# Four edits to a two-layer metaformer kernel: the last image in two halves, additions in place of reductions, a residual by load, and first loads in another order

## The chip, the cores and the metric

The kernel runs on one core of a Trainium2 chip. The metric is the device time of one execution in microseconds, lower is better. A core has five engines with a queue of instructions each: PE (TensorE, matrix products into PSUM), DVE (VectorE), ACT (ScalarE), POOL (GpSimd) and SP (SyncE, which only issues transfers here). Each works through its own queue in order and waits on semaphores of the others. Transfers (DMA) are issued from SP, ACT or POOL.

## What is computed

x is 8 x 128 x 32 x 32 in fp32: 8 images, 128 channels, 1024 positions ("tokens"). Two layers, each with a mixer and a feed-forward part, both with a residual:

```python
# layer 0
x = x + attention(_ln_c(x))                  # 8 heads, softmax over 1024 tokens
t = _to_tokens(x)
t = t + stu(_ln_t(t))                        # causal convolution with 16 spectral filters, then
x = _from_tokens(t, x)                       # einsum('btkd,k,kde->bte'), plus 3 lags; 4 resolutions
# layer 1
x = x + deformable_conv(_ln_c(x))            # per token 3 taps, each 4 corners, bilinear weights and a mask
t = _to_tokens(x)
t = t + experts(_ln_t(t))                    # softmax router over 8 experts, the best 2, normalised
x = _from_tokens(t, x)
```

In the deformable convolution a tap reads four table rows at computed places and adds them with weights:

```python
samp = gather(iy0, ix0) * (1 - wy) * (1 - wx) + gather(iy0, ix0 + 1) * (1 - wy) * wx + ...
samp = samp * mask[:, j][..., None]
out = out + jnp.einsum('bhwc,oc->bohw', samp, conv_w[:, :, 0, j])
```

## The kernel before

**Stages.** Attention for all 8 images comes first. Then `spectral_and_second_layer` runs the STU of layer 0 and, interleaved with it by hand, layer 1. The order of instructions on each engine is the order in which this Python code emits them.

**The STU.** The work is a list of 128 units (8 images x 16 filters). For each unit `filter_image` makes the convolution (products `p_x`, `p_y`, `p_z` on PE, put together by ACT, POOL and DVE into `us`), and two units later `mix` multiplies `us` by the filter's matrix `mf` and adds the product into `po`, an accumulator in PSUM that holds one image. `start_sums` opens `po` at the first filter of an image: 8 products with `flip`, a reversed identity, put the residual x1 into it (L1437, with the matmul in `add`, L1453). `x1` holds the image's tokens in reversed order; a gather brings it in `prepare` (L1391), and two buffers alternate. At an image's end `finish` copies `po` into `x2`, one half on ACT (L1529), one on DVE (L1530).

Before the first unit SP issues, in this order, the filters of units 1 and 2 (`teto`, L1257 and L1258), the matrices of the lags (`mu`, L1322) and the parts of the first mixing matrix (`m_room`, L1366). From `m_room` POOL forms `both` (L1371, L1372), and from it DVE the matrix `mf` (L1379, L1381). `setup` of layer 1 then loads small weights, the last step of which adds a bias to the table of base positions (L906).

**Layer 1.** The class `DeformAndExperts` has two generators. Each `yield` hands back an amount of time, and after each half of a unit `advance(RATE)` lets the generators go on by 3.2 such units (`LAST_RATE`, 3.6, during the last image). `points` turns the image back to tokens (`turn_back`: 4 transposes into a PSUM bank, a copy by ACT to `tok`, L1168 and L1169; twice), normalises it (`norm_steps`, with `inverse_std`: three Newton steps in small instructions), turns it again (L919), multiplies by the taps' weights (`p_g`, L1025), copies to `gs` on ACT (L1028) and writes `gs` to a table in DRAM, 24 writes of 256 KB (L1018): 3 taps x 4 corners x 2 halves of the image. Offsets and masks (`p_om`, `corners`) give the row numbers and the weights `w`. `sampled` then works on tiles of 128 tokens, 8 for an image. For a tile 3 gathers (L1077, by POOL) bring 12 x 128 values into `g`; taps 0 and 1 are weighted on ACT (L1095, 8 instructions), tap 2 on DVE (L1099); then DVE adds up the 12 parts and `tok`:

```python
nc.vector.tensor_reduce(x3[:, i, :], g.rearrange("p t k c -> p c (t k)"), AX.X, ALU.add)   # L1103
nc.vector.tensor_add(x3[:, i, :], x3[:, i, :], tok[:, i, :])                               # L1106
```

After the 8 tiles come a normalisation, a turn (L919), the router (`gates`: logits `p_l` L1180 on PE, about 20 small instructions on DVE, L1186 to L1209) and, tile by tile, the experts: two products `p_e` (L1123), gates on four experts by ACT (L1130) and four by DVE (L1135), the sum of 8 parts by a reduction (L1140) and an addition (L1143). After four tiles a bank `p_out` (L1152, L1155) is copied to `ot`, and at the end one transfer writes the image (L1160). Tiles `g` of both steps share three buffers.

The layer-1 work of an image runs behind its STU, inside the STU of the next one. For the last image there is no next one: after the last unit a loop lets `layer.image(B - 1, ...)` run alternately with what is left of the rows. There `alone` is true: the Newton steps are on DVE instead of POOL, and every second table write is issued by ACT (L1017).

Of the kernel before, what the change touches and what calls it, by code (L numbers as in the profile page):

```python
# [11 lines left out]
F32 = mybir.dt.float32  # L12
I32 = mybir.dt.int32
# [5 lines left out]
P = 128  # L19
# [16 lines left out]
LAST_RATE = 3.6  # L36
# [726 lines left out]
def inverse_std(nc, pool, var, eps, newton):  # L763


    v = pool.tile([P, NT], F32, tag="rs_v", name="rs_v", bufs=2)
    y = pool.tile([P, NT], F32, tag="rs_y", name="rs_y", bufs=2)
    t = pool.tile([P, NT], F32, tag="rs_t", name="rs_t", bufs=2)
    bits = pool.tile([P, NT], I32, tag="rs_b", name="rs_b", bufs=2)
# [33 lines left out]
class DeformAndExperts:  # L803
# [4 lines left out]
    def __init__(  # L808
        self, ctx, tc, ident, dram, conv_w, conv_b, off_w, off_b, mask_w, mask_b,
# [6 lines left out]
        self.ident, self.dram, self.out = ident, dram, out  # L816
# [4 lines left out]
    def setup(self):  # L821
# [13 lines left out]
        bias = cp.tile([P, 9], F32, name="bias")  # L835
# [64 lines left out]
        for i in range(NT):  # L900
# [5 lines left out]
        nc.vector.tensor_tensor(  # L906
            self.base, self.base, bias.unsqueeze(1).to_broadcast([P, NT, 9]), ALU.add
# [17 lines left out]
    def first_max(self, e, name):  # L925

        nc = self.nc
        top = self.sb.tile([P, NT], F32, tag="top", name=f"top_{name}")
        oh = self.sb.tile([P, NT, NE], F32, tag=f"oh_{name}", name=f"oh_{name}")
        nc.vector.tensor_reduce(top, e, AX.X, ALU.max)  # L930
        nc.vector.tensor_tensor(oh, e, top.unsqueeze(2).to_broadcast([P, NT, NE]), ALU.is_equal)
        nc.vector.scalar_tensor_tensor(oh, oh, -64.0, self.eidx, ALU.mult, ALU.add)
        nc.vector.tensor_reduce(top, oh, AX.X, ALU.min)
        nc.vector.tensor_tensor(oh, oh, top.unsqueeze(2).to_broadcast([P, NT, NE]), ALU.is_equal)
        return oh
# [49 lines left out]
    def image(self, b, x2):  # L985

        got = []
        yield from self.points(b, x2, got, True)
        yield from self.sampled(b, got, True)

    def points(self, b, x2, got, alone):
# [5 lines left out]
        yield from self.turn_back(x2, tok)  # L997
# [15 lines left out]
        def write():  # L1013
            if writes:
                i0, tap, slot, back = writes.pop(0)
                r0 = 33 - back + i0 * P
                queue = nc.scalar if alone and slot % 2 else nc.sync  # L1017
                queue.dma_start(  # L1018
# [37 lines left out]
    def sampled(self, b, got, alone):  # L1056
# [4 lines left out]
        newton = nc.vector if alone else nc.gpsimd  # L1061
# [4 lines left out]
        fetched, here, tiles = [], [], []  # L1066

# [22 lines left out]
        for i, tap in points:  # L1090
# [7 lines left out]
            else:  # L1098
# [4 lines left out]
                nc.vector.tensor_reduce(  # L1103
                    x3[:, i, :], g.rearrange("p t k c -> p c (t k)"), AX.X, ALU.add
                )
                nc.vector.tensor_add(x3[:, i, :], x3[:, i, :], tok[:, i, :])  # L1106
            yield 1.7 if alone else 2.6
        tt = sb.tile([P, NT, C], F32, tag="ht", name="tt")
        yield from norm_steps(nc, sb, x3, tt, 1e-5, newton, not alone)
        yield 1.0 if alone else 5.0  # L1110
# [4 lines left out]
        yield from self.gates(tc, got, 0.0 if alone else 3.0)  # L1115
        gate, gt = got
        ot = sb.tile([C, T], F32, tag="ht", name="ot")
        for i in range(NT):
            g = sb.tile([P, TAPS, 4, C], F32, tag="g", name="ge", bufs=3)
            part = g.rearrange("p t k c -> p (t k) c")[:, 0:NE]  # L1120
            for grp in range(2):
# [12 lines left out]
                else:  # L1134
# [4 lines left out]
                    both = sb.tile([P, C], F32, tag="both", name="both")  # L1139
                    nc.vector.tensor_reduce(  # L1140
                        both, part.rearrange("p e c -> p c e"), AX.X, ALU.add
                    )
                    nc.vector.tensor_add(x3[:, i, :], x3[:, i, :], both)  # L1143
                yield 1.3 if alone else 2.2
            if i % 4 == 3:
# [12 lines left out]
                nc.scalar.copy(ot[:, half * 512 : half * 512 + 512], po)  # L1158
                yield
        nc.sync.dma_start(self.out[b].rearrange("c h w -> c (h w)"), ot)  # L1160

    def turn_back(self, src, dst):

        for half in range(2):
            pt = self.bank("p_back")
            for i in range(4):
                t0 = (half * 4 + i) * P
                self.nc.tensor.transpose(pt[:, i * P : (i + 1) * P], src[:, t0 : t0 + P], self.ident)  # L1168
            self.nc.scalar.copy(  # L1169
                dst[:, half * 4 : half * 4 + 4, :].rearrange("p a c -> p (a c)"), pt  # L1170
            )
            yield

    def gates(self, tt, got, wait):


        nc, sb = self.nc, self.sb
        pl = self.bank("p_l")
        for i in range(NT):
            nc.tensor.matmul(  # L1180
                pl[:, i * NE : (i + 1) * NE], tt[:, i * P : (i + 1) * P], self.rw,
                start=True, stop=True,
            )
        yield
        e = sb.tile([P, NT, NE], F32, tag="ge", name="ge")
        nc.vector.tensor_tensor(  # L1186
            e, pl[:, 0 : NT * NE].rearrange("p (i e) -> p i e", e=NE),
            self.rb.unsqueeze(1).to_broadcast([P, NT, NE]), ALU.add,
        )
        mx = sb.tile([P, NT], F32, tag="mx", name="mx")  # L1190
        nc.vector.tensor_reduce(mx, e, AX.X, ALU.max)
        nc.vector.tensor_tensor(e, e, mx.unsqueeze(2).to_broadcast([P, NT, NE]), ALU.subtract)
# [3 lines left out]
        oh1 = self.first_max(e, "a")  # L1196
        e2 = sb.tile([P, NT, NE], F32, tag="e2", name="e2")
        nc.vector.scalar_tensor_tensor(e2, oh1, -2.0, e, ALU.mult, ALU.add)
        yield
        oh2 = self.first_max(e2, "b")  # L1200
# [3 lines left out]
        nc.gpsimd.memset(gates[:, NT:, :], 0.0)  # L1204
        gate = gates[:, 0:NT, :]
# [3 lines left out]
        nc.vector.tensor_tensor(gate, gate, mx.unsqueeze(2).to_broadcast([P, NT, NE]), ALU.mult)  # L1209
# [323 lines left out]
def spectral_and_second_layer(tc, spec, layer, weights):  # L1533
# [5 lines left out]

    mf = {}  # L1540
    parts = spec.load_parts(0)
    both = None

# [183 lines left out]
```

## Time and profile before

| | us |
|---|---|
| median of 3 runs (lowest, highest) | 2700.72 (2695.61, 2702.18) |
| the profiled execution | 2699.79 |
| its span, first to last instruction | 2698.0 |
| PE busy | 2530.0 (94%) |
| DVE busy | 1852.9 (69%) |
| POOL busy | 1448.6 (54%) |
| ACT busy | 1083.5 (40%) |
| PE's first product of the STU starts | 913.5 |
| copy of the last image's `po` (ACT) starts | 2559.6 |

The profile gives groups of instructions (line, engine, operation, tiles, count, busy time and mean duration, idle time before them and what ended it), a timeline in order of time, windows with the busy time of each engine, and waits. A line number in it is a line of the kernel before. A fp32 product counts as two matmuls in these rows, so "x16" stands for 8 products. "PEclk" and "granted clock" are the share of PE's full clock that was granted.

### The profile page before, as it was taken

The page shows a single profiled execution, that of the slowest core. Times are in us where ns is not written, and L with a number is a line of the kernel's source. Part 1 is how long each engine was busy: PE and PEld are TensorE (multiplying, and loading weights), DVE is VectorE, ACT ScalarE, POOL GpSimd, SP SyncE. Part 2 cuts the span into 40 slices and gives each one's busy share as a digit, 9 for nine tenths or more (in the row PEclk, how much of TensorE's full clock was granted, in tenths as well). Part 3 has the DMA queues.
Part 4 walks back from the last instruction along what each step waited for, and adds up shares of the span by engine and source line. Part 5 has one row for each costly group of instructions (what it writes and reads, how often), then busy time and mean ns, then how long its engine had stood idle before and what let it go on. Part 6 is the DMA issues. An engine that isn't in the chain of part 4 may idle for free. (4 is left out here: it accounts for less than half of the span.)

```text
span 2698.0 us, 47432 instructions
## 1 busy us (share of the span) xinstructions
PE 2530.0 (94%) x18896; PEld 1769.3 (66%) x18896; DVE 1852.9 (69%) x2728; ACT 1083.5 (40%) x2030; POOL 1448.6 (54%) x1535
## 2 busy tenths in 40 slices
PE   6999999999999799999999999999999999999924
PEld 3555555555555578777787787778778778777712
DVE  3888888888888455448648649648648657658646
ACT  4666766667667111123223224224214224224232
POOL 4777777777788455446246237237236227226230
PEclk9999999999999899999999999999999999999956
DMA  1000000000000254375275266265266266256151
GB/s 29 2 17 2 17 17 2 17 9 10 9 17 17 83 162 153 119 207 160 73 212 169 71 198 184 71 191 176 79 181 194 71 173 194 79 149 202 40 168 35
DMA packets 204675, 267.10 MB, mean 99 GB/s; under 512 B 20308, under 2 KB 138260, under 8 KB 204448
## 3 DMA queue, kind: packets, MB, share of 16 engines
q1 hardware_dynamic: 181312, 205.27, 26.1%
q0 software_dynamic: 16800, 55.59, 6.2%
q10 hardware_dynamic: 6336, 3.15, 0.4%
q8 instruction: 151, 2.47, 0.4%
q14 instruction: 76, 0.62, 0.1%
HBM read 196.02 MB, written 67.92 MB: 98 GB/s over the span
## 5 line engine op out<-in xcount | busy, mean ns | idle before, releaser
L623 POOL TENSOR_TENSOR t<-e 128x1024 f32<-128x1024 f32 x256 | 608.3, 2376 | 199.3 <-ACT e L614 199.0
L651 DVE TENSOR_TENSOR e<-e,rb 128x2048 f32<-128x2048 f32 x256 | 570.8, 2278 | 84.1 <-PE rb L644 84.1
L614 ACT ACTIVATE e<-s 128x2048 f32<-128x2048 f32 x256 | 481.2, 1880 | 253.2 <-PE s L609 250.7
L1501 POOL TENSOR_TENSOR part<-us,part 128x256 f32<-128x256 f32 x256 | 189.9, 743 | 708.5 <-ACT part L1500 707.8
L1453 PE MATMUL po<-us,mf 128*128 128x128 f32 (+2 forms) x2048 | 528.9, 381 | 5.9 <-DVE mf L1381 3.8
L1506 DVE TENSOR_TENSOR part<-p_y,part 128x512 f32<-128x512 f32 x256 | 175.4, 685 | 310.0 <-PE p_y L1488 193.2
L1499 ACT COPY us<-p_x 128x256 f32<-128x256 f32 x256 | 94.8, 370 | 723.2 <-PE p_x L1488 712.8
L1453 PEld LDWEIGHTS po<-us,mf 128*128 128x128 f32 x2048 | 308.2, 191 | 37.5 <-issue 4.8
L609 PE MATMUL s<-q,k 32*128 32x256 f32 x4096 | 296.1, 403 | 14.5 <-ACT e L614 13.7
L661 PE MATMUL av<-e,vt 128*32 128x256 f32 x4096 | 287.9, 388 | 5.3 <-DVE e L651 4.0
L1516 DVE TENSOR_TENSOR us<-p_z,part 128x512 f32<-128x512 f32 x256 | 174.8, 683 | 151.7 <-PE p_z L1488 151.3
L1488 PEld LDWEIGHTS p_z<-diff,gap 128*128 128x128 f32 x1024 | 193.1, 191 | 129.6 <-issue 88.3
L609 PEld LDWEIGHTS s<-q,k 32*128 32x128 f32 x4096 | 186.4, 185 | 137.5 <-ACT e L614 116.3
L1488 PE MATMUL p_z<-diff,gap 128*128 128x256 f32 x1024 | 266.1, 382 | 3.6 <-DVE base L906 3.1
L1095 ACT ACTIVATE g<-g,w 128x128 f32<-128x128 f32 x512 | 161.2, 393 | 118.1 <-DMA g<-tab,here 91.1
L1077 POOL DMA_INDIRECT g<-tab,here x168 | 167.3, 996 | 71.8 <-issue 31.6
L661 PEld LDWEIGHTS av<-e,vt 128*32 128x32 f32 x4096 | 101.3, 109 | 142.2 <-issue 84.3
L1103 DVE TENSOR_REDUCE x<-g 128x128 f32<-128x1536 f32 x64 | 180.4, 2819 | 7.5 <-ACT g L1095 1.5
L1239 POOL TENSOR_TENSOR diff<-teto 128x516 f32<-128x516 f32 x127 | 163.6, 1288 | 1.6 <-DMA teto<-in_phi_o 0.8
L637 DVE RECIPROCAL r<-z 128x256 f32<-128x256 f32 x64 | 112.5, 1757 | 69.5 <-PE z L630 69.3
L1488 PE MATMUL p_y<-diff,gap 128*128 128x256 f32 x512 | 152.6, 379 | 0.1
L1488 PE MATMUL p_z<-teto,ht 128*128 128x256 f32 x512 | 132.3, 381 | 0.0
(264 smaller groups left out, 3731.9 us busy)
## 6 DMA issues: line engine op xcount, KB each, us to landing
mf<-mfd SPq DMA_DIRECT2D x112, 512.0 KB
tab<-gs SPq DMA_DIRECT2D x180, 256.0 KB
teto<-in_phi_o SPq DMA_DIRECT2D x127, 256.5 KB
teto<-in_phi_e SPq DMA_DIRECT2D x127, 256.0 KB
mfd<-mf SPq DMA_DIRECT2D x16, 512.0 KB
xc<-in_x SPq DMA_DIRECT2D x8, 512.0 KB
x1d<-xt SPq DMA_DIRECT2D x8, 512.0 KB
m_room<-in_M_plus SPq DMA_DIRECT2D x16, 256.0 KB
```

The source lines that it names most:

```text
L609: nc.tensor.matmul(s[:, j, c, :], img["k"][rows, hg, 2 * r + c, :], q[rows, qc * QU : (qc + 1) * QU], start=True, stop=True,)
L614: nc.scalar.activation(e.rearrange("p j c q -> p (j c q)"), s.rearrange("p j c q -> p (j c q)"), AF.Exp, scale=float(HD) ** -0.5,)
L623: nc.gpsimd.tensor_add(t, e[:, :, 0, :], e[:, :, 1, :])
L651: nc.vector.tensor_tensor(e, e, un["rb"].unsqueeze(2).to_broadcast([P, NH, 2, QU]), ALU.mult)
L661: nc.tensor.matmul(qrt["av"][32 * j : 32 * j + 32, 0:QU], img["v"][:, 2 * r + c, P * hg + 32 * j : P * hg + 32 * j + 32], un["e", r][:, j, ...
L1077: nc.gpsimd.indirect_dma_start(out=tiles[-1][:, tap].rearrange("p k c -> p (k c)"), out_offset=None, in_=rows, in_offset=bass.IndirectOffs ...
L1103: nc.vector.tensor_reduce(x3[:, i, :], g.rearrange("p t k c -> p c (t k)"), AX.X, ALU.add)
L1453: self.nc.tensor.matmul(out, lhsT, rhs, start=bank not in img["opened"], stop=last, skip_group_check=True)
L1488: nc.tensor.matmul(out, weights, moving, start=start, stop=stop, skip_group_check=True)
L1501: nc.gpsimd.tensor_add(part[:, 0], mine[:, :, 0:P], part[:, 1])
L1506: nc.vector.tensor_tensor(part[:, 2:4], y[:, 0].unsqueeze(1).to_broadcast([C, 2, 2, P]), part[:, 0:2], ALU.add)
L1516: nc.vector.tensor_tensor(result(2, 4), z, part[:, 2:4], ALU.add)
```

## The change

1. `start_sums` no longer multiplies x1 into `po`. Instead `residual` loads the image's x1 from DRAM in token order with 4 transfers on SP, three filters before the image's end, into a tile `x1n` with one buffer, and `turn_back` adds it on DVE while it empties the PSUM bank (before: a copy by ACT). `x1` has one buffer in place of two.
2. In `sampled` and `experts` the reductions over 12 and 8 parts become additions: `add_up` adds the upper half of the parts onto the lower (6 and 3 parts, or 4 and 2), then `three`, or two additions, give the result with `tok` or `x3`.
3. The last image: after each tile's sum DVE takes the statistics; after four tiles `last_half` is started and advances by one step beside each tap of the tiles that follow (normalisation, turn, gates and experts for four tiles). The second half runs after the last tile. Its gates are made in a tile of their own; all table writes go to SP; the yields with `alone` lose their amounts.
4. `experts` is now a method; each half of `ot` is written to `out` when it has been copied.
5. First loads: `load_parts(0)` comes first, then filter 1, x1 of image 0, the lags and filter 2. The addition of L906 moves from the end of `setup` to a generator `settle`, which is queued at unit 1.
6. `LAST_RATE` is 3.8.

```diff
-LAST_RATE = 3.6
+LAST_RATE = 3.8
...
-def inverse_std(nc, pool, var, eps, newton):
+def inverse_std(nc, pool, var, eps, newton, width=NT):
...
+    def residual(self, b):
+        x1 = self.sb.tile([P, NT, C], F32, tag="x1n", name="x1n", bufs=1)
+        got = x1.rearrange("q (i two) c -> q two i c", two=2)
+        for half in range(2):
+            src = self.x1d[b, 64 * half : 64 * half + 64].rearrange(
+                "p (par i) c -> p par i c", par=2
+            )
+            for par in range(2):
+                self.nc.sync.dma_start(got[par:P:2, half], src[:, par])
+        return x1
...
-                queue = nc.scalar if alone and slot % 2 else nc.sync
-                queue.dma_start(
+                nc.sync.dma_start(
...
-                nc.vector.tensor_reduce(
-                    x3[:, i, :], g.rearrange("p t k c -> p c (t k)"), AX.X, ALU.add
-                )
-                nc.vector.tensor_add(x3[:, i, :], x3[:, i, :], tok[:, i, :])
-            yield 1.7 if alone else 2.6
+                self.add_up(g.rearrange("p t k c -> p (t k) c"), (6, 3))
+                self.three(x3[:, i, :], g[:, 0, 0:3], tok[:, i, :])
+            if not alone:
+                yield 2.6
+                continue
+            if tap == TAPS - 1:
+                nc.vector.bn_stats(st[:, i, :], x3[:, i, :])
+                nc.vector.bn_aggr(mv[:, i, :], st[:, i, :])
+                if i % 4 == 3:
+                    later.append(
+                        self.last_half(b, x3, mv, tt, tc, ot, range(i - 3, i + 1))
+                    )
+            if later and next(later[0], later) is later:
+                later.popleft()
+            yield
+        if alone:
+            while later:
+                later.append(later.popleft())
+                if next(later[0], later) is later:
+                    later.popleft()
+                yield
+            return
...
+    def last_half(self, b, x3, mv, tt, tc, ot, tiles):
+        nc, lo, n = self.nc, tiles[0], len(tiles)
+        mine = slice(lo, lo + n)
+        rs = inverse_std(nc, self.sb, mv[:, mine, 1], 1e-5, nc.vector, n)
+        for i in tiles:
+            nc.vector.tensor_scalar(
+                tt[:, i, :], x3[:, i, :], mv[:, i, 0:1], rs[:, i - lo : i - lo + 1],
+                ALU.subtract, ALU.mult,
+            )
+        pt = self.bank("p_turn")
+        for i in tiles:
+            nc.tensor.transpose(pt[:, (i - lo) * P : (i - lo + 1) * P], tt[:, i, :], self.ident)
+        nc.scalar.copy(tc[:, lo * P : (lo + n) * P], pt[:, 0 : n * P])
+        got = []
+        yield from self.gates(tc, got, 0.0, tiles)
+        yield from self.experts(b, tc, x3, ot, *got, tiles)
...
-                    nc.vector.tensor_reduce(
-                        both, part.rearrange("p e c -> p c e"), AX.X, ALU.add
-                    )
-                    nc.vector.tensor_add(x3[:, i, :], x3[:, i, :], both)
-                yield 1.3 if alone else 2.2
+                    self.add_up(part, (4, 2))
+                    for k in range(2):
+                        nc.vector.tensor_add(x3[:, i, :], x3[:, i, :], part[:, k])
+                yield 2.2
...
+                nc.scalar.copy(ot[:, cols], po)
+                nc.sync.dma_start(self.out[b].rearrange("c h w -> c (h w)")[:, cols], ot[:, cols])
...
+    def add_up(self, parts, counts):
+        for n in counts:
+            self.nc.vector.tensor_add(parts[:, 0:n], parts[:, 0:n], parts[:, n : 2 * n])
+
+    def three(self, out, parts, more):
+        self.nc.vector.tensor_add(out, parts[:, 0], more)
+        for k in (1, 2):
+            self.nc.vector.tensor_add(out, out, parts[:, k])
...
-    def turn_back(self, src, dst):
+    def turn_back(self, src, dst, more):
...
-            self.nc.scalar.copy(
-                dst[:, half * 4 : half * 4 + 4, :].rearrange("p a c -> p (a c)"), pt
-            )
+            part = [t[:, half * 4 : half * 4 + 4, :].rearrange("p a c -> p (a c)") for t in (dst, more)]
+            self.nc.vector.tensor_tensor(part[0], pt, part[1], ALU.add)
...
-        img["x1"] = sb.tile([P, NT, C], F32, tag="x1", name="x1", bufs=2)
+        img["x1"] = sb.tile([P, NT, C], F32, tag="x1", name="x1")
...
-        for par in range(2):
-            for i in range(4):
-                out = po[:, i // 2, par, (i % 2) * P : (i % 2 + 1) * P]
-                self.add(img, i // 2, out, img["x1"][:, par * 4 + i, :], self.flip)
...
-    imgs = {0: spec.prepare(0)}
-    filters = {0: spec.given.filter, 1: spec.load_filter(1), 2: spec.load_filter(2)}
-    less = {0: spec.given.given.diff}
-    spec.load_lags()
     mf = {}
     parts = spec.load_parts(0)
     both = None
+    filters = {0: spec.given.filter, 1: spec.load_filter(1)}
+    less = {0: spec.given.given.diff}
+    imgs = {0: spec.prepare(0)}
+    spec.load_lags()
+    filters[2] = spec.load_filter(2)
...
+                    if src == 1 and slot == 0 and k == NF - 3:
+                        img["tokens"] = layer.residual(img["b"])
```

## Prediction

> **What bounds the kernel now.** I read the page's slices first, for the stages.
>
> ```profile
> PE   6999999999999799999999999999999999999924
> DVE  3888888888888455448648649648648657658646
> PEclk9999999999999899999999999999999999999956
> ```
>
> A slice is 67.5 us. Attention fills thirteen slices, the STU runs from the dip (913 us) to about 2560 us, and the last two slices are a tail in which PE is nearly idle. From 972 to 2560 us the windows give PE 1566.8 busy of 1588 us at a granted clock of 0.98 to 1.00: the STU costs what PE's instructions cost. The groups and the timeline price what is edited there:
>
> ```profile
> L1103 DVE TENSOR_REDUCE x<-g 128x128 f32<-128x1536 f32 x64 | 180.4, 2819 | 7.5 <-ACT g L1095 1.5 <-issue 0.5
> L1140 DVE TENSOR_REDUCE both<-ge 128x128 f32<-128x1024 f32 x64 | 122.8, 1919 | 6.2
> L1106 DVE TENSOR_TENSOR x<-x,tok 128x128 f32<-128x128 f32 x64 | 30.4, 474 | 2.3
> L1143 DVE TENSOR_TENSOR x<-x,both 128x128 f32<-128x128 f32 x64 | 23.8, 372 | 2.2
> ```
> ```profile
> 1120.81 1.95 PE L1453 MATMUL po<-flip,x 128*128 128x128 f32 x16
> 1122.60 1.04 PE L1453 MATMUL po<-us,mf 128*128 128x128 f32 x6
> ```
>
> Then the tail, by the timeline of each engine. It is a chain of waits: writes of the table, gathers, DVE work, and DVE stalls on a cold PE.
>
> ```profile
> 2567.62 0.28 DVE L788 BATCH_NORM_STATS2 st<-tok 128x6 f32<-128x128 f32 x1
> 2581.21 17.15 SPq L1018 DMA_DIRECT2D tab<-gs  x12
> 2588.53 10.17 ACTq L1018 DMA_DIRECT2D tab<-gs  x6
> 2606.20 1.05 POOL L1077 DMA_INDIRECT g<-tab,cn_idx  x1 [27.61 <-issue]
> 2612.51 0.69 DVE L1099 TENSOR_TENSOR g<-g,w 128x512 f32<-128x512 f32 x1 [12.03 <-DMA g<-tab,cn_idx]
> 2655.81 0.22 DVE L1186 TENSOR_TENSOR ge<-p_l,rb 128x64 f32<-128x64 f32 x1 [3.80 <-PE p_l L1180]
> 2664.74 0.69 DVE L1135 TENSOR_TENSOR ge<-p_e,gates 128x512 f32<-128x512 f32 x1 [3.81 <-PE p_e L1123]
> 2680.85 0.69 DVE L1135 TENSOR_TENSOR ge<-p_e,gates 128x512 f32<-128x512 f32 x1 [4.30 <-PE p_e L1123]
> ```
>
> From here on the old lines are named, unless a line is said to be new.
>
> **1. Residual out of the STU: -12.5 us.** The 16 flip passes start at 1120.81 and the next matmul at 1122.60: 1.79 us of PE an image. Seven images lie wholly in the PE-bound stretch: 7 x 1.79 = 12.5. In exchange SP issues four loads an image (about 0.43 us each by its neighbours, 1.7 us) and DVE's addition out of PSUM (0.69 by L1530's 0.69 copy) takes the place of ACT's copy (0.59). I cost these at nothing: SP has pauses of 13 us between units (three loads from 2319 to 2320, the next at 2332.7), the filters are read three units (some 35 us) ahead, and the residual is asked for two units before its use. Without that cover a unit starts 1.7 us late, 14 us in all. The load's tile is free since the image before was turned back. The output's second DMA adds 0.35 us of SP.
>
> **2. First loads: -1.0 us (0 to -4).** PE stood from 930.12 to 933.92: POOL's `both` began at 927.21 because m_room had landed behind eight other loads on SP. With m_room first, POOL can start about when the filters let it now (920.59) plus two subtractions (2 us) and some landing, say 923.5, so `mf` comes some 3.8 us earlier and this gap closes; image 0's flips disappear in it. But the next unit's m_room stays behind the same small weight loads on SP (issued 932.05, used by POOL 940.91), and PE waits until 945.29 for what follows it. That wait is late next and should take most back. Moving L906 (`settle`) takes 0.22 us of DVE out of the 951.6 wait; L1506 and L1509 end there anyhow, so nothing.
>
> **3. Earlier end of image 6: +4.4 and -5.1 us.** In the new order none of image 6 is left behind the STU. Before, three expert matmuls (6 passes of 0.43 = 2.6) and one output group (16 passes, 1.8) ran after the last `po`; now PE does them before it: +4.4. In exchange DVE no longer works through two experts of image 6 between 2561.8 and 2567.6. Its two additions can follow p_back at 2560.96 and 2561.85, and the statistics start at about 2562.5 instead of 2567.62: -5.1.
>
> **4. Additions for reductions, alone.** A DVE add costs 0.292 at 128 elements and 0.696 at 512 (tail rows of L1106, L1099), so 0.965 at 768, 0.56 at 384, 0.43 at 256; a dependent instruction starts 0.03 later, a free one 0.08 earlier. A sampled tile: 0.78 + 0.995 + 0.59 + 3 x 0.32 + statistics 0.42 = 3.74, against 0.78 + 2.79 + 0.21 + 0.39 = 4.17. An expert tile: 0.785 + 0.725 + 0.46 + 0.32 + 0.21 = 2.50 against 2.96. In the tail that is 8 x (0.43 + 0.46) = 7.1 us of DVE saved. In the STU I count nothing, since DVE has 557 us spare there. "VectorE: DVE Perf Modes" of the Trainium skill (the perf-mode tier table) gives tensor_reduce the same one element a cycle as fp32 tensor_tensor. An estimate by that page's (N+151)/0.96 makes the 1536-element reduction 1.76 us, and five adds would then lose some 0.3 us a tile. The row has 2.75 us in the tail, and I go by it.
>
> **5. The last image in halves: -1.5 us.** Twice the inverse square root (15 small instructions, 3.05 more) and twice the gates (19 of 0.255 become 38 of about 0.225: 3.7 more) give back 6.8 of the 7.1: -0.3. What remains are stalls, in DVE's own queue. Before, from 2612.51 on: 0.6 + 3.8 + 0.3 + 3.8 + 4.3 = 12.8. After: tiles 0 to 3 arrive as now (0.8). The first half's L1186 stands in front of tile 4, whose multiplication and everything later wait for turn 0.56 + copy 0.6 + 0.2 + 8 passes of 0.215 = 3.0. In the second half tile 2's expert product stands behind turn and logits on PE: 3.07 + two cold passes of 0.8 = 4.7. The last experts wait for p_gt and p_e as at 2664.74: 3.8. Sum 12.3: -0.5. ACT and POOL (a memset of 0.17 between gathers) run ahead of DVE by then. The last output DMA is half as large; its data took 1.5 us: -0.7. Bounds: if PE were warm, the 11.5 us of matmul stalls could halve (-5); if every two-input add delayed a gather as the one at 2612.62 was (1.41 instead of 0.96), the twelve gathers up to tile 3 add +5.
>
> **6. All table writes on SP: -2.5 us (-4.1 to +3).** The end is when the 6.3 MB have landed: 22.9 us at 275 to 290 GB/s with two queues. One queue ran at 345 GB/s in image 5's writes (2416 to 2423): 18.2 us plus a start of 0.6, -4.1. But those 24 writes, with three loads among them, took 28.1 us from first issue (2401.27) to gather (2429.34), against 25.0 in the tail: +3. The loads were 1.28 of 7.57 MB, so I take a value nearer the first. ACT's copies stop waiting for DMA issues (4.5 us), which is hidden: SP reaches the second half's writes later still.
>
> **Sum.** -12.5 - 1.0 + 4.4 - 5.1 - 1.5 - 2.5 = -18.2. The profiled execution took 2699.79 (span 2698.0), the median of the runs is 2700.72: 2681.6 and 2682.5; I say 2682. With the bounds of 2, 5 and 6 and up to 5 us of new waits in the STU, this case spans 2672 to 2692.
>
> **Rivals.** *The adds meet POOL (slower).* L1106 has a minimum of 0.291, a mean of 0.50 and a maximum of 1.95 in the STU, while the reductions hardly vary (2.79 to 2.88): two-input adds wait for POOL. Five per sampled tile at 0.21 and four per expert tile at L1143's 0.10 are 1.45 x 56 = 81 us of waiting. DVE alone would absorb it, since alone its adds save 56 x (0.72 + 0.50) = 68 us. But POOL's `part` (L1501) feeds L1506, and if a third came through to PE, 27 us: 2709. It decides from 0.16 us of PE idle per tile (18.2 over 112 tiles). Against it: today's 2.8 us reductions block DVE for longer at a stretch, and PE loses only 21 us in all. "SBUF — State Buffer" (SBUF: two separate sides) speaks for it: a DVE instruction with two SBUF inputs and a GpSimd one that reads SBUF take turns for their whole length. *One queue is slow (no change).* SP's own pace in the tail was 17.15 / 12 = 1.43 us; 24 of these end 16.8 us later than now: 2682 + 19.3 = 2701. Against it: SP alone issued 8 in 6.53 us at 2401. *The flips' time is not returned (no change):* PE then waits at the same place for `us` or for the emptied bank: 2682 + 12.5 = 2694.5. Against it: `po` had been emptied by 1117.7, three us ahead. *More gain:* first loads -4, writes -4.1, warm PE -5: 2682 - 9.6 = 2672, and less if the STU also waits less.
>
> **Chances.** Forecast 0.55, more gain (2660 to 2672) 0.13, a mixture of small losses still over 0.3% better 0.09, flips or queue without effect 0.11, port 0.12. A difference under 0.3% (8.1 us) can't be told from none here. Faster 0.77, same 0.11, slower 0.12. The range 2662 to 2697 leaves out the port's case and the outer end of more gain.
>
> **What will show it.** The flip group gone, and PE's next `po` 1.8 us earlier in each image; PE idle in the STU still about 21 us; the gap at 945 us still there; statistics of the last image some 3 us after PE's last `po`; all table writes between first issue and gather in 22 to 23 us; DVE stalls of about 3, 4.7 and 3.8 us in the tail; sampled tiles of 3.7 us. The prediction is wrong if PE's idle time in the STU grows by over 15 us, if the writes take over 30 us, or if adds of 768 elements cost over 1.2 us in the tail.

## The result and the profile after

The changed kernel takes 2699.93 us (median of 12 runs), the kernel before 2700.23 beside it: the ratio is 0.9996, with a 95% interval of 0.9984 to 1.0007. Nothing can be told from none; 2682 had been predicted. The profiled execution of the changed kernel takes 2702.7 us, its span is 2701.0. Line numbers in this section are those of the changed kernel, unless it says before; with an experiment they are those of its own kernel.

Over the whole page only POOL is busier (1480.6 us, 1448.6 before). Two stages have moved, in opposite directions. The copy of the last image's `po` by ACT starts at 2567.1 us instead of 2559.6: the STU, forecast 9.1 us shorter (terms 1 to 3), is 7.5 longer. From there to the end it takes 133.9 instead of 138.4 us: 4.5 shorter, where 9.1 were forecast. So 16.6 us are missing in the STU and 4.6 in the tail.

Most of the 16.6 is idle time of PE. Between the first and the last of the eight copies of `po`, PE's idle time grows by 14.0 us (20.8 before, 34.8 after). Its busy time falls by 6.3 us there, where 8.1 were forecast (12.5 less 4.4), and the first copy is 0.2 us earlier, where 1.0 was forecast. The granted clock is not the cause: by an estimate from windows of 2 us (one less the granted clock, times PE's busy time) it costs 5.0 us of this stretch before and 4.6 after.

In the STU the flips are gone, and in every image PE reaches the next `po` 1.79 us earlier, as forecast. But while `sampled` runs for the image before, that lead is lost: about half of it in the first of the seven stretches between copies (199.3 us, 200.2 before), all of it and more in the others (the second takes 209.0 us, 206.7 before). The waits of PE between 972 and 2546 us (who waited for whom, us in total, times, longest), before and after:

```profile
PE p_turn L919 <- DVE tt L795: 10.1, 18, 1.0
...
PE po L1453 <- DVE us L1516: 2.1, 1, 2.1
...
PE p_y L1488 <- DVE us L1516: 0.9, 2, 0.5
```
```profile
PE p_turn L924 <- DVE tt L795: 13.0, 20, 1.0
PE po L1519 <- DVE us L1575: 7.9, 6, 1.5
PE po L1519 <- DVE us L1582: 5.2, 3, 2.8
...
PE p_z L1554 <- DVE us L1575: 1.8, 5, 0.4
```

PE waited 3.0 us for `us` before and 14.9 after. The same window of both kernels, before first (first column the window, then its length, the busy time of PE, PE's weight loads, DVE, ACT and POOL with numbers of instructions, then PE's granted clock and the DMA's share and rate):

```profile
972.00:2546.00 1574.00, 1553.19 (x7193) 1220.90 (x7192) 1023.57 (x1971) 440.21 (x1369) 717.31 (x988) 1.00 0.49 148
```
```profile
972.00:2546.00 1574.00, 1539.19 (x7062) 1205.22 (x7061) 1023.67 (x2259) 433.64 (x1357) 746.36 (x987) 1.00 0.50 150
```

DVE's busy time is the same to 0.1 us (1023.6 and 1023.7), so it is not more work over the whole STU that makes `us` late. One such place in the timeline of the changed kernel (start, duration, engine, line; what is in brackets is the idle time before):

```profile
1452.46 2.31 DVE L1224 TENSOR_TENSOR g<-g 128x768 f32<-128x768 f32 x2
...
1452.92 2.42 POOL L1567 TENSOR_TENSOR part<-us,part 128x256 f32<-128x256 f32 x2
...
1454.80 1.94 DVE L1228 TENSOR_TENSOR x<-g,tok 128x128 f32<-128x128 f32 x1
...
1455.32 1.27 POOL L1309 TENSOR_TENSOR diff<-teto 128x516 f32<-128x516 f32 x1
...
1456.78 1.03 DVE L1230 TENSOR_TENSOR x<-x,g 128x128 f32<-128x128 f32 x2
...
1458.32 0.41 DVE L1575 TENSOR_TENSOR us<-p_y,part 128x256 f32<-128x256 f32 x1
...
1458.79 0.70 PE L1519 MATMUL po<-us,mf 128*128 128x256 f32 x2 [1.28 <-DVE us L1575]
```

DVE's two additions and POOL's two overlap and both take longer than alone: from 1452.46 to 1455.34 it is 2.88 us for 1.52 (0.96 + 0.56) on DVE and about 1.48 (2 x 0.74) on POOL. The two sums are 3.00 us: they take turns. L1228, 0.29 us alone, lasts 1.94, until POOL's subtraction is done. The `us` of that half unit stands behind all this in DVE's queue, and PE waits for it. The groups by form show it over the whole STU (972 to 2546 us): the reduction and its addition before, the additions after, and then four tiles of the changed kernel's tail (2616 to 2637 us), where POOL only gathers:

```profile
L1103 DVE TENSOR_REDUCE x<-g 128x128 f32<-128x1536 f32 x56 | 158.4, 2829 | 6.8 <-ACT g L1095 1.5 <-issue 0.5
...
L1106 DVE TENSOR_TENSOR x<-x,tok 128x128 f32<-128x128 f32 x56 | 28.0, 500 | 1.9
```
```profile
L1224 DVE TENSOR_TENSOR g<-g 128x768 f32<-128x768 f32 x56 | 94.4, 1685 | 5.4 <-issue 0.4
L1224 DVE TENSOR_TENSOR g<-g 128x384 f32<-128x384 f32 x56 | 40.2, 718 | 1.9
...
L1228 DVE TENSOR_TENSOR x<-g,tok 128x128 f32<-128x128 f32 x56 | 27.1, 483 | 1.9
```
```profile
L1224 DVE TENSOR_TENSOR g<-g 128x768 f32<-128x768 f32 x4 | 3.8, 959 | 0.4
...
L1228 DVE TENSOR_TENSOR x<-g,tok 128x128 f32<-128x128 f32 x4 | 1.2, 292 | 0.2
```

The first addition takes 1685 ns in the STU and 959 alone. With the weighting (L1121, 872) and two of 314 a sampled tile is 872 + 1685 + 718 + 483 + 628 = 4386 ns of DVE; with the reduction it was 876 + 2829 + 500 = 4205. The step that should have made DVE's work shorter made it 0.18 us a tile longer (10.1 us for 56 tiles), and irregular. In `experts`, by the same groups, a tile's sum did become shorter: 693 + 433 + 2 x 311 = 1748 ns, where the reduction and its addition took 1923 + 390 = 2313. What this costs, and why, the experiments had to show.

### The profile page after: what moved, and what is told of

It is laid out like the page before. It is cut to its first block, busy times and chain, and to the rows that moved or that the text cites. A ratio compares the mean times of both kernels' runs of the same rounds, so it can differ in the third digit from the quotient of the medians.

```text
span 2701.0 us, 47627 instructions
## 1 busy us (share of the span) xinstructions
PE 2521.4 (93%) x18769; PEld 1755.3 (65%) x18769; DVE 1848.9 (68%) x3099; ACT 1075.1 (40%) x2016; POOL 1480.6 (55%) x1536
## 5 line engine op out<-in xcount | busy, mean ns | idle before, releaser
L623 POOL TENSOR_TENSOR t<-e 128x1024 f32<-128x1024 f32 x256 | 608.4, 2376 | 199.3 <-ACT e L614 199.0
L1567 POOL TENSOR_TENSOR part<-us,part 128x256 f32<-128x256 f32 x256 | 201.4, 788 | 688.0 <-ACT part L1566 687.5
L609 PE MATMUL s<-q,k 32*128 32x256 f32 x4096 | 296.1, 403 | 14.6 <-ACT e L614 13.8
L1554 PEld LDWEIGHTS p_z<-diff,gap 128*128 128x128 f32 x1024 | 193.3, 191 | 129.8 <-issue 95.7
L1099 POOL DMA_INDIRECT g<-tab,here x168 | 180.1, 1072 | 69.5 <-issue 32.7
L1224 DVE TENSOR_TENSOR g<-g 128x768 f32<-128x768 f32 (+1 forms) x128 | 146.7, 1146 | 8.4 <-issue 0.4
```

The lines of the kernel that those rows point to most:

```text
L609: nc.tensor.matmul(s[:, j, c, :], img["k"][rows, hg, 2 * r + c, :], q[rows, qc * QU : (qc + 1) * QU], start=True, stop=True,)
L623: nc.gpsimd.tensor_add(t, e[:, :, 0, :], e[:, :, 1, :])
L1099: nc.gpsimd.indirect_dma_start(out=tiles[-1][:, tap].rearrange("p k c -> p (k c)"), out_offset=None, in_=rows, in_offset=bass.IndirectOffs ...
L1554: nc.tensor.matmul(out, weights, moving, start=start, stop=stop, skip_group_check=True)
L1567: nc.gpsimd.tensor_add(part[:, 0], mine[:, :, 0:P], part[:, 1])
```

## The experiments

Twelve kernels ran, each in five rounds beside the kernel before. "Stretches" is the time from the first to the last of the eight copies of `po` by ACT (seven images), "tail" from the last copy to the end, both from one profiled execution. Kernels with the same code there differ by some 5 to 8 us (residual alone, additions at the end and first loads: 1426.1, 1430.7 and 1434.5). By the estimate from windows of 2 us the granted clock costs 1.7, 4.8 and 8.1 us of these three, which is most of the difference. So smaller differences of single stretches are not read.

| kernel | median us | ratio to before (95%) | stretches | tail |
|---|---|---|---|---|
| before | 2699.5 to 2702.9 | 1 | 1443.3 | 138.4 |
| changed | 2699.9 | 0.9996 (0.9984 to 1.0007) | 1451.0 | 133.9 |
| reductions in the STU | 2685.4 | 0.9942 (0.9926 to 0.9957) | 1437.0 | 132.9 |
| the same, `sampled` only | 2684.3 | 0.9934 (0.9918 to 0.9951) | 1438.8 | 132.9 |
| residual alone | 2681.2 | 0.9931 (0.9914 to 0.9949) | 1426.1 | 138.2 |
| additions alone | 2709.0 | 1.0038 (1.0025 to 1.0050) | 1460.1 | 134.8 |
| last rate 3.6 | 2685.3 | 0.9940 (0.9924 to 0.9955) | 1432.4 | 137.9 |
| idle additions | 2772.3 | 1.0260 (1.0244 to 1.0276) | | |
| idle reductions | 2767.1 | 1.0244 (1.0226 to 1.0261) | | |
| two queues | 2686.1 | 0.9945 (0.9930 to 0.9961) | 1435.9 | 133.4 |
| additions at the end | 2681.4 | 0.9922 (0.9908 to 0.9935) | 1430.7 | 135.5 |
| spread | 2685.9 | 0.9941 (0.9927 to 0.9955) | 1440.9 | 132.9 |
| first loads | 2683.7 | 0.9930 (0.9916 to 0.9943) | 1434.5 | 139.3 |
| whole and even | 2686.9 | 0.9952 (0.9935 to 0.9969) | 1445.2 | 128.7 |

### Which part loses the time

**Reductions in the STU.** The changed kernel, with the old sums while the STU runs:

```diff
-                self.add_up(g.rearrange("p t k c -> p (t k) c"), (6, 3))
-                self.three(x3[:, i, :], g[:, 0, 0:3], tok[:, i, :])
+                if alone:
+                    self.add_up(...)
+                    self.three(...)
+                else:
+                    nc.vector.tensor_reduce(
+                        x3[:, i, :], g.rearrange("p t k c -> p c (t k)"), AX.X, ALU.add
+                    )
+                    nc.vector.tensor_add(x3[:, i, :], x3[:, i, :], tok[:, i, :])
```

(and the same with `part` in `experts`)

> The changed kernel with the reductions of before in `sampled` and `experts` while the STU runs; the last image keeps its additions. Theory (additions meet POOL): the two-input additions of DVE and POOL's work delay each other in the STU, `us` comes late and PE waits. The copy of the last image's `po` then starts at 2551 to 2555 us instead of 2567.1, the recurring waits of PE for `us` (18 us in the STU) fall below 6 us, and the whole takes 2684 to 2688. Rival (flips' time not returned): PE waits for `us` at the same places whatever DVE's sums look like; the copy stays at 2566 to 2568, the whole at 2699 to 2702. Rival (residual): the residual's load and its addition on DVE delay the rows; the same, 2699 to 2702.

2685.41 us, 14.5 below the changed kernel's median; the last copy starts at 2546.3, some 5 us earlier than the theory said (this execution began the STU 3.3 us earlier). PE's waits for `us` fall from 14.9 to 4.7 us in the same window. The additions in the STU are the part that takes the gain back.

**`sampled` only.** The same without the edit in `experts`.

> The changed kernel with the reduction of before in `sampled` alone while the STU runs; `experts` keeps its additions. Theory (additions meet POOL): the additions over 768 and 384 elements took 1202 ns on the mean in the STU and about 760 alone, those over 512 and 256 elements 563 and 560, so nearly all of the loss is in `sampled`: within 2 us of the kernel with both reductions, 2684 to 2690. If `experts` carries the loss as well: 2691 to 2697. Rivals (flips or residual): 2699 to 2702.

2684.25 us: no difference to both. In `experts` the additions cost nothing that shows, and the time that they save on DVE there brings nothing either. The loss is made in `sampled`.

**Residual alone.** The kernel before with `residual`, `turn_back` and `start_sums` of the change:

```diff
-        for par in range(2):
-            for i in range(4):
-                out = po[:, i // 2, par, (i % 2) * P : (i % 2 + 1) * P]
-                self.add(img, i // 2, out, img["x1"][:, par * 4 + i, :], self.flip)
...
+                    if src == 1 and slot == 0 and k == NF - 3:
+                        img["tokens"] = layer.residual(img["b"])
...
-            self.nc.scalar.copy(...)
+            self.nc.vector.tensor_tensor(part[0], pt, part[1], ALU.add)
```

> The kernel before with the residual's part of the change alone (load of x1 by SP, addition on DVE in turn_back, no flips, one buffer x1); reductions, tail and first loads as before. Theory (additions meet POOL): nothing takes the flips' 12.5 us back, so 2686 to 2690, and the copy of the last `po` starts at 2546 to 2549. Rivals (flips not returned, or residual delays the rows): 2697 to 2702, copy at 2556 to 2561.

2681.24 us, a ratio of 0.9931 (0.9914 to 0.9949): 13.8 to 23.2 us faster. The flips' time is returned in full, and the whole gains more than the 12.5 us of the forecast; the load and the addition on DVE cost nothing that shows. The last copy starts at 2536.7, earlier than either theory said, partly since this execution began the STU 3 us earlier.

**Additions alone.** The kernel before with `add_up` and `three` (or two additions) in place of both reductions, in the STU and in the tail.

> The kernel before with the additions in place of both reductions and nothing else. Theory (additions meet POOL): the STU loses 12 to 17 us (copy of the last `po` at 2571 to 2577), the tail gains about 7 by shorter DVE work: 2705 to 2711. Rivals (flips or residual): the STU is as before (copy at 2559 to 2561) and the tail gains 7: 2692 to 2695.

2708.95 us. The last copy starts at 2576.0, 16.4 later than before, and the tail is 3.6 shorter instead of 7. The loss does not need the rest of the change.

### Collisions, or DVE's time?

Two kernels put some 90 us of idle work into DVE's queue, behind the sum of each sampled tile in the STU, on top of the first experiment. One adds with two operands, the other reduces one:

```diff
                     nc.vector.tensor_add(x3[:, i, :], x3[:, i, :], tok[:, i, :])
+                    self.add_up(g.rearrange("p t k c -> p (t k) c"), (6, 3))
```
```diff
                     nc.vector.tensor_add(x3[:, i, :], x3[:, i, :], tok[:, i, :])
+                    idle = sb.tile([P, C], F32, tag="both", name="idle")
+                    nc.vector.tensor_reduce(
+                        idle[:, 0:72], g[:, :, :, 0:72].rearrange("p t k c -> p c (t k)"),
+                        AX.X, ALU.add,
+                    )
```

> The first experiment (reductions back in the STU) with two additions more behind each sampled tile in the STU, in place on parts of `g` that nobody reads again (768 and 384 elements, 1.55 us alone): 56 x 1.55 = 87 us more DVE work. Theory (additions meet POOL): 10 to 17 us slower than the first experiment, 2695 to 2702, and POOL's `part` goes from 741 to about 790 ns. Rival (DVE's time alone): as the next kernel, whose additional DVE time is the same.

> The first experiment with one reduction more behind each sampled tile in the STU (864 of its elements, result unread, about 1.58 us): 56 x 1.58 = 88 us more DVE work, with one operand. Theory (additions meet POOL): 0 to 5 us slower than the first experiment, 2685 to 2690, POOL's `part` stays at 741 ns. Rival (DVE's time alone): as slow as the kernel with additions more, 2695 to 2702.

Both theories missed. The additions cost 86.9 us against the first experiment, the reductions 81.7. What was put in measures 95.7 us (1027 + 682 ns a tile) and 91.5 us (1634 ns), so about nine tenths of DVE's additional time arrive in the total, whatever its kind, and 4.2 of the 5.2 us between the two are DVE's own. The collisions are there in the first alone, as the theory said: POOL's `part` takes 769 ns beside the additions and 742 beside the reductions. They bring no price of their own that shows. The windows suggest why (columns as above). Two windows of the kernel before, in `sampled` and behind it:

```profile
1412.00:1464.00 52.00, 52.00 (x247) 42.37 (x246) 47.08 (x54) 24.73 (x83) 39.60 (x43) 1.00 0.67 199
1260.00:1330.00 70.00, 67.66 (x312) 50.85 (x311) 46.93 (x95) 17.78 (x54) 20.10 (x34) 1.00 0.25 79
```

The changed kernel, then the kernel with idle reductions, in `sampled`:

```profile
1410.00:1465.00 55.00, 53.32 (x254) 43.36 (x253) 49.87 (x80) 24.86 (x82) 42.68 (x43) 1.00 0.63 188
```
```profile
1420.00:1481.00 61.00, 53.40 (x250) 42.23 (x248) 60.01 (x59) 24.49 (x80) 39.12 (x43) 1.00 0.56 168
```

In `sampled` DVE was busy 47.1 of 52 us (91%), behind it 67%. The 557 us that DVE has to spare lie elsewhere. 1.6 us more a tile fill the stretch to 98%, and DVE is the bound. In the changed kernel DVE is 91% busy too, but its additions vary by what POOL does (L1228 takes 0.29 us alone and 1.94 in the timeline above). One reading is that the regular reductions just fitted and the irregular additions don't; how much of the loss is their irregularity and how much the 10.1 us by which the tiles are longer, no run separates. On either reading the same additions must be harmless where the tiles stand further apart.

**Spread.** The changed kernel with two yields altered:

```diff
-                yield 2.6
+                yield 3.0
...
-                yield 2.2
+                yield 1.6
```

> The changed kernel with its additions, only the rate of two steps altered: `sampled` yields 3.0 per tap in place of 2.6, so that its 8 tiles take a longer stretch of the STU, and `experts` yields 1.6 in place of 2.2, so that the row takes as long as before. In `sampled`'s stretch DVE was 91% busy (before 1412 to 1464: 47.1 of 52 us), behind it 67%; two more operations of 1.6 us a tile made it 98% and cost 85 us of 87. Theory (the loss is DVE's local saturation there, which collisions with POOL tip over): spread, the same additions cost less: the seven stretches between copies of `po` sum to 1434 to 1443 us instead of 1451, the whole 2684 to 2693. Rival (each collision costs PE wherever it stands): 1448 to 1453, the whole 2697 to 2703.

2685.94 us: 14 us come back though every addition is still there. In 1410 to 1480 us PE is busy all 70.0 us, DVE 61.3 (88%). Yet they still collide: the first two additions of a tile take 1038 ns on the mean (1202 in the changed kernel, 758 alone), those of `experts` 698 where they took 563, and POOL's `part`, 742 ns before the change and 789 after, is at 800 (198.4 us in all):

```profile
L1224 DVE TENSOR_TENSOR g<-g 128x768 f32<-128x768 f32 x112 | 116.2, 1038 | 7.4 <-issue 0.4
```

So the collisions alone don't set the price. That they cost where DVE has no slack left fits the windows, but it is argued: the shift moves `experts` too, and the same shift with reductions was not run. Between the first and the last copy PE's idle time is 24.1 us, where it was 34.8. The waits of PE from 1120 to 2530 us show that the crowd has moved to the end of the image, where `experts` is now denser and the copy of `po` stands behind its additions:

```profile
PE p_back L1238 <- DVE x L1596: 14.4, 5, 3.1
...
PE p_z L1554 <- DVE us L1575: 0.4, 1, 0.4
```

These waits cost more than their length. From 1508 to 1520 us the granted clock is 0.72 on the mean, where the changed kernel has 1.00 around its own copy (1518 to 1532 us), and over the seven stretches the products into `p_out` take 0.33 us each instead of 0.28. By the estimate from windows of 2 us the clock costs 14.0 us of its stretches.

### The other terms

**Last rate 3.6.** The first experiment with `LAST_RATE = 3.6`.

> The changed kernel with the reductions back in the STU (the first experiment, 2685.4 us) and LAST_RATE 3.6 as before. In that experiment the last image's stretch between two copies of `po` took 208.5 us, in the kernel before with the residual alone 201.3, and the tail 132.9 against 138.2. Theory (the rate only moves layer-1 work of image 6 from behind the last product to before it): the last stretch falls to 202 to 204, the tail grows by 3 to 6, the whole 2683 to 2687. Rival (the rate makes the rows crowd, and PE waits for it): the stretch falls by 6 or more, the tail grows by under 2, the whole 2679 to 2682.

2685.26 us: no difference. The last stretch falls from 208.5 to 204.5, the tail grows from 132.9 to 137.9: work of image 6 is moved, not saved. The three other kernels with 3.6 and the residual have 201.3 to 204.6 in that stretch, the two others with 3.8 and reductions in `sampled` 208.7 and 208.9.

**Two queues.** The first experiment with every second table write of the last image on ACT's queue (`queue = nc.scalar if alone and slot % 2 else nc.sync`).

> The first experiment with the last image's table writes on two queues again (every second one from ACT). In the traces of before and after the time from first write to first gather is 25.0 and 25.1 us. Theory (the end of the writes is set by what all transfers move together): 24 to 26 us here too, the whole within 2 us of 2685.4. Rival (SP's issues alone set it, and two queues only looked the same because of other loads): 21 to 23 us, the whole 2681 to 2683.

2686.11 us, and 25.4 us from first write to first gather, against 24.9 with one queue. With this transfer, one queue and two take the same time.

**First loads.** Residual alone, with the order of loads and `settle` of the change.

> The kernel before with the residual's part (2681.2 us), the first loads in the changed order and `settle`. Theory (the matrix's parts now come first, but the filter of unit 1 lands late, POOL's differences hold `both` back, and only 0.5 us is gained): PE's wait for the first `mf` stays within 1.5 us of the kernel without it, the whole within 2.5 us of 2681.2. Rival (the order itself delays later units): the whole 2684 to 2687, and the first copy of `po` 3 us or more later against the STU's first product.

2683.73 us, at the edge of what was expected, and no difference by the ratios. PE's wait for `mf` falls from 5.1 to 3.8 us, and its waits at `p_x` and `p_ut` grow by 1.1 and 2.0. Part of that is the start: PE's first product of the STU comes at 912.9 us here and at 910.5 in the residual alone. In the changed kernel one reads the cause on POOL:

```profile
924.79 1.28 POOL L1309 TENSOR_TENSOR diff<-teto 128x516 f32<-128x516 f32 x1 [4.36 <-DMA teto<-in_phi_o]
...
926.71 1.27 POOL L1441 TENSOR_TENSOR both<-m_room 128x512 f32<-128x512 f32 x1
```

The parts of the matrix are there, but the filter now lands behind them, and POOL's queue takes its differences first: `both` starts at 926.71 instead of 927.21, and the STU's first product at 912.7 instead of 913.5, so against that start nothing is gained.

**Additions at the end.** Residual alone, with the additions in the last image only, which stays whole.

> The kernel before with the residual's part (2681.2 us) and additions for reductions in the last image alone, which stays whole: no halves, all else as before. In the kernel before with additions the stretch from the first weighted tile of the last image to the end took 82.1 us, in before 85.5, in the changed kernel 85.7, and in the changed kernel with reductions in the STU and LAST_RATE 3.6 84.8 (2685.3 us). Theory (additions help the tail, the halves give it back): 81.5 to 82.5 us there, the whole 2676 to 2680. Rival (halves and additions each bring what I predicted, and something else of the change costs it): 84 to 86 us there, the whole 2680 to 2683.

81.9 us from the first weighted tile to the end, as the theory had it; the whole, 2681.41, can't be told from the residual alone and lies in the rival's range. DVE's busy time there falls by 8.7 us (63.8 to 55.1), the length by 3.6 (85.5 to 81.9). The rest turns into waits, one at each tile:

```profile
2606.44 0.69 DVE L1111 TENSOR_TENSOR g<-g,w 128x512 f32<-128x512 f32 x1 [1.11 <-DMA g<-tab,cn_idx]
```

Seven such waits make 6.1 us: a tile's three gathers, 0.95 to 1.46 us each with 0.30 between, now take longer than DVE. The halves fill these waits with other work, but their second set of small instructions brings DVE back to 61.3 us, and PE's products, slow there (granted clock 0.64 on the mean), stay in the way. DVE's waits in the changed kernel's tail:

```profile
2639.66 0.19 DVE L1256 TENSOR_TENSOR ge<-p_l,rb 128x32 f32<-128x32 f32 x1 [3.12 <-PE p_l L1250]
...
2673.11 0.69 DVE L1195 TENSOR_TENSOR ge<-p_e,gates 128x512 f32<-128x512 f32 x1 [5.02 <-PE p_e L1183]
...
2686.34 0.69 DVE L1195 TENSOR_TENSOR ge<-p_e,gates 128x512 f32<-128x512 f32 x1 [4.04 <-PE p_e L1183]
```

So the stretch takes 85.7 us with halves and 81.9 without. DVE waits 1.4 us for gathers instead of 6.1, and 12.2 for PE instead of 10.1.

**Whole and even.** A try for more: residual, additions everywhere, the last image whole, and yields between the two extremes.

```diff
-LAST_RATE = 3.6
+LAST_RATE = 3.8
...
-            yield 1.7 if alone else 2.6
+            yield 1.7 if alone else 2.8
...
-                yield 1.3 if alone else 2.2
+                yield 1.3 if alone else 1.9
```

> The kernel before with the residual's part and the additions everywhere, the last image whole, first loads and table writes as before, LAST_RATE 3.8; `sampled` yields 2.8 per tap in the STU (2.6 before) and `experts` 1.9 (2.2 before), so that the row is as long as before. The kernel with 3.0 and 1.6 lost its waits for `us` but waited 14.4 us for the copy of `po`, behind the additions of `experts` at the end of the image. Theory (DVE must be short of saturation in both steps, collisions or not): PE's waits for `us` and for that copy sum to under 12 us between 1120 and 2530 us (2.2 + 14.4 us with 3.0 and 1.6, some 15 in the changed kernel), the seven stretches to 1431 to 1437, the tail 128 to 131, the whole 2670 to 2678, below the residual alone (2681.2). Rival (additions in `sampled` cost PE at any rate below 3.0): waits for `us` of 12 us or more, stretches of 1442 or more, the whole 2684 to 2694.

The waits it was about are down to 5.1 us (`us` 4.0, the copy 1.1), and the tail is 128.7. But the whole is 2686.88 and the stretches are 1445.2: theory and rival both missed, the theory by the time and the rival by the waits, for two other waits have grown in their place (PE, 1120 to 2530 us):

```profile
PE p_gt L1233 <- DVE gates L1227: 13.2, 7, 2.1
PE p_y L1502 <- POOL diff L1257: 8.9, 6, 4.0
```

The shifted row now puts the turn of the gates in front of PE before DVE has them, and work on POOL in front of the filter's differences. Rates that avoid all four places at once were not tried. The best versions that ran are the residual alone and the same with additions at the end or with the first loads, all some 19 to 21 us below before by their ratios.

## Why the prediction was wrong

**The step that failed** is in part 4: "In the STU I count nothing, since DVE has 557 us spare there." It cost 14.5 us (2699.9 - 2685.4), of some 18 by which the forecast missed. The spare time was an average over the whole STU. In `sampled`'s stretch, a quarter of each image, DVE was 91% busy, and one window there would have shown it. In its place the runs show that a tile's additions take 3.51 us there (2.39 alone) where reduction and addition took 3.33, that PE's waits for `us` grow from 3.0 to 14.9 us, and that they fall to 4.7 when the reductions are back.

**The rival "adds meet POOL"** was right in its row: two-input additions last longer beside POOL, and its 1.05 us a sampled tile measure 1.12. Its price, 27 us from an assumed third of 81, was too high, and its place was too wide: `experts`, counted with 0.10 us for each of four additions, costs nothing. Its path was another one: DVE's waits for POOL's `part` are 84.4 us before and 83.6 after, and `us` comes late in DVE's own queue. What I held against it was wrong too: that DVE would absorb the waiting is so for the total (1023.6 and 1023.7 us) and not for `sampled`, and that PE lost only 21 us beside the reductions said nothing of the additions. The page "SBUF — State Buffer" of the Trainium skill (SBUF: two separate sides), cited for it, states that a DVE instruction with two SBUF inputs and a GpSimd one that reads SBUF exclude each other for a whole instruction. The timeline at 1452 us agrees: L1228 lasts 1.94 us, until POOL's subtraction is done. The prediction's sign of failure, 15 us more of PE idle time in the STU, was nearly met: from 972 to 2546 us it is 20.8 before and 34.8 after.

**1. Residual, -12.5:** right for the STU, and the main gain. The three kernels with this code in the STU and reductions (residual alone, additions at the end, first loads) have stretches 17.2, 12.6 and 8.8 us shorter than before, 12.9 on the mean, and PE's busy time in them is 12.9 us lower on the mean as well. The whole gains more: 18.6 us in the run alone, with an interval from 13.8. A part of the rest lies before the first copy, which comes 2.6 to 5.8 us earlier in these three; how much of that is image 0's flips, which I had at nothing, no run separates.

**2. First loads, -1.0:** about nothing. I reckoned that POOL could start when "the filters let it now", but the filter's own load had been moved behind m_room. The gap at 945 us is there still, as said.

**3. Earlier end of image 6, +4.4 and -5.1:** right in both; the last stretch is 4.0 longer with the higher rate, the tail 5.0 shorter.

**4. Additions in the tail, 7.1 us of DVE:** right for DVE alone (8.7), and 0.959 us for 768 elements where 0.965 was said. The estimate from "VectorE: DVE Perf Modes" of the Trainium skill (the perf-mode tier table), 1.76 us for the reduction of 1536 elements, is too low here. The tail's rows have 2.75 us, and they decide. But only 3.6 us of it reach the end, for the gathers are next in line: I had counted 0.8 us of waits for them up to tile 3, and their delay by additions as a bound only.

**5. Halves, -1.5:** the stalls were said to be 3.0, 4.7 and 3.8 and are 3.1, 5.0 and 4.0. What was missed is that a whole image with additions would have been the better one: the halves spend 6.1 us of DVE, close to the 6.8 said, to fill 4.7 of 6.1 us of waits for gathers, and wait 2.1 us longer for PE. Against before the stretch is 0.2 longer.

**6. One queue, -2.5:** nothing; 25.1 us against 25.0. The rate of 345 GB/s, read in 7 us of an earlier stage, did not carry over, and the rival "one queue is slow" was wrong as well.

## What to carry to other kernels

Read spare time of an engine in the windows of the stage in which work is added, not over the whole: a bound of 99% PE can hide a DVE that is 91% busy in a quarter of the time. There, instructions that are shorter alone can be longer beside another engine and cost what they were to save; spread over a longer stretch, the same ones gave 14 us back here. And a row of yields moves waits as easily as it removes them: after a shift every wait has to be read again, those of other engines too.

## What the hardware showed that was not expected

A reduction over the strided view of 12 parts takes 2.83 us for 1536 elements beside POOL and 2.75 without, whereas an addition of 768 elements takes 0.96 alone and 1.69 on the mean beside it. DVE's additions with one operand in PSUM (`us`, 683 ns before and 684 after) are not lengthened either. POOL pays too: in the STU beside the additions its gathers take 1072 ns instead of 996 and `part` 789 instead of 742.
